# Four graph layers in one launch: when four small loads start, and how the last half of the last layer ends

## The chip, the cores and the metric

The kernel runs on one core of one Trainium2 chip. The metric is the device time of one execution in microseconds (us), and of several executions the median. Before the change it is 2736.38 us, the median of three runs (2735.53 to 2736.8).

## What is computed

Eight graphs (batch B = 8) of N = 2048 nodes with C = 128 features share one adjacency matrix of 2048 x 2048 whole numbers. Four layers follow each other, each on the layer-normed and rectified features, and each adds its output to x. Layers 0, 1 and 3 are graph attention with one score per pair of nodes, layer 2 is attention with four heads and no weights. Cut to what matters here:

```
for layer in 0, 1, 2, 3:
    h = max(layernorm(x), 0)
    x = x + gnn[layer](h, adj)

gnn[3](h):
    h = h * node_weights[n] + node_bias[n] + h
    h = layernorm(h @ W) * gamma + beta
    e = leaky_relu(s1[i] + s2[j], 0.2) where adj[i, j] > 0, else -9e15
    return elu(softmax(e) @ h + h)
```

The four vectors `node_weights`, `node_bias`, `gamma` and `beta` belong to layer 3 alone.

## The kernel before

**Layout.** A graph's x is a tile of 128 partitions x 16 blocks x 128 features. The adjacency is turned once, at the start, into a tile `edge` of bytes (16 blocks of 128 x 2048). Attention runs in *tokens*: for a block `jb` of 128 source nodes and a *half* of 1024 target nodes, VectorE makes the masked weights `zg` (128 x 1024, three buffers; `front`, L758), and PE adds them, in eight groups of 128 columns with two instructions each, against the rows `y` into PSUM (`back`, L767). Column 128 of `y` is a weight, so that the sum by which to divide comes out beside the features. A half has 16 tokens. When the last is done, `out` (L787) divides and ends the half.

**Order.** The instructions of the fast path are put in order by the program itself, one order for each engine. A planner (`Plan`, L171) takes operations with an engine, an estimated duration, a due time, needs, and buffers that they take and free. It simulates them: at each step it takes the engine that can start first, and on it, among the operations that can start within 0.148 us of the first one, that with the lowest due time (a front with free `zg` buffers is ranked 54.8 us earlier). The result is only the order in which each engine gets its instructions. On the chip an engine runs its own in order, and an instruction waits only for the data and buffers that it uses itself. A need that stands in the plan alone is no wait on the chip.

**The start.** SP issues the first graph's x in four loads and then 16 blocks of the adjacency of 1 MB each (L370). Seven buffers take them: five of `z`, two of `m`. VectorE turns each into a block of `edge` (L373), which frees its buffer. Meanwhile the first graph is normed, projected (L590) and its tokens begin (from 29 us). Three more x loads follow the blocks on SP, and ScalarE subtracts 2 from each (L433).

Small loads are issued by GpSimd. `load_weights` (L279) takes weights. `load_more` (L295) takes the four vectors of layer 3: two as 128 x 16 numbers, element by element (`nw1_sb`, `nb_sb`), and two that are spread over all partitions (`gamma_sb`, `beta2_sb`). In the plan it needs the last block of `edge`, `rows_in[NB - 1]` (L1167). The first instructions that read what it loads are at the end of `projections(3)`, in `bounded` (L345, L346), which add 1 to the node weights and double `beta`. `symmetry(j)` (L379) tests on PE and ScalarE that the adjacency is symmetric: block row j against blocks 0 to j of `edge`, and the squares of the differences are summed. In the plan it needs `rows_in[j]`.

**The end of a half in layer 3.** `divided` (L792) takes three banks of PSUM in turn: the reciprocal of the sums (L799), then features times it into `oa` (L800). `rows3` (L811) takes the rows of `y` times `cr[2]`, which gives the normed rows before gamma and beta, into `oe`. `wide3` (L818) adds them to `oa`, multiplies by gamma and adds `beta2_sb`, twice beta, over all 1024 columns. Then ScalarE makes Exp of it into `oe` and Relu in place (L806), and VectorE adds `min(oe, 1)` (L830) and `oa` (L833) to x; the constant -1 that is left over is in x already. SP writes the half to HBM (L925). In halves of the other graphs some of these adds are DMAs of GpSimd (L884, L836). The last half of all is graph 7, half 1; the half before it, graph 7, half 0, shares its buffers `oa` and `oe`, of which there is one each.

Of the kernel before, what the change touches and what calls it, by code (L numbers as in the profile page):

```python
# [8 lines left out]
F32 = mybir.dt.float32  # L9
# [5 lines left out]
AF = mybir.ActivationFunctionType  # L15
OP = mybir.AluOpType
# [4 lines left out]
P = 128  # L21
# [19 lines left out]
def adj_preln_d4(ctx: ExitStack, tc: tile.TileContext, x, adj, w0, a0, w1, a1, w3, a3,  # L41
# [17 lines left out]
    nc = tc.nc  # L59
    B, N, C = x.shape  # L60
    NB = N // P
    HB = NB // 2
    NG = NB // 4
    CE = C + 1
    HN = N // 2
# [16 lines left out]
    edge = const.tile([P, NB, N], U8, name="edge")  # L82
# [9 lines left out]
    nw1_sb = const.tile([P, NB], F32, name="nw1_sb")  # L92
    nb_sb = const.tile([P, NB], F32, name="nb_sb")
    gamma_sb = const.tile([P, C], F32, name="gamma_sb")
    beta2_sb = const.tile([P, C], F32, name="beta2_sb")
# [75 lines left out]
    class Plan:  # L171
# [11 lines left out]
        def add(self, engine, us, due, emit, needs=(), takes=(), frees=(), lag=None, tiled=False):  # L183
            op = Op(engine, us, due, emit, needs, takes, frees, self.LAG[engine] if lag is None else lag, tiled)
            self.ops.append(op)
            return op
# [56 lines left out]
    def fast(ctx):  # L243
        stat = ctx.enter_context(tc.tile_pool(name="stat", bufs=3))
        big = ctx.enter_context(tc.tile_pool(name="big", bufs=2))
        dram = ctx.enter_context(tc.tile_pool(name="dram", bufs=2, space=DRAM))
        ps = ctx.enter_context(tc.tile_pool(name="psum", bufs=1, space=PSUM)).tile(
            [P, 8, 512], F32, name="ps")
# [7 lines left out]
        add = plan.add  # L256
# [36 lines left out]
            load(out=beta_col, in_=beta.rearrange("(p o) -> p o", o=1))  # L293

        def load_more(op):  # L295
            load = nc.gpsimd.dma_start
            load(out=nw1_sb, in_=node_w.rearrange("(n p) -> p n", p=P))
            load(out=nb_sb, in_=node_b.rearrange("(n p) -> p n", p=P))
            load(out=gamma_sb, in_=gamma.partition_broadcast(P))
            load(out=beta2_sb, in_=beta.partition_broadcast(P))  # L300
# [61 lines left out]
        rows_in, squares, loaded = [], [], []  # L362
# [16 lines left out]
        def symmetry(j):  # L379

            wide = (j + 1) * P
            for k in range(0, wide, 512):
                w, n = min(512, wide - k), len(squares)

                def differences(op, k=k, w=w):
                    pv = ps[:, op.got["pair"], :]
                    nc.tensor.matmul(pv[:, :w], lhsT=minus_8, rhs=edge_8[:, j, k:k + w],
                                     start=True, stop=False, skip_group_check=True)
                    for i in range(k // P, (k + w) // P):
                        at = i * P - k  # L390
                        nc.tensor.matmul(pv[:, at:at + P], lhsT=edge_8[:, i, j * P:(j + 1) * P],
                                         rhs=plus_8, start=False, stop=i == (k + w) // P - 1,
                                         skip_group_check=True)

                due = 115.0 + 9.0 * j
                last = add("PE", 0.1 + 0.1 * w / P, due, differences, [rows_in[j], *units[0, 0].v_ready], takes=["pair"])
                squares.append(add("ACT", 0.6, due, lambda op, w=w, n=n, last=last: nc.scalar.activation(
                    ps[:, last.got["pair"], :w], ps[:, last.got["pair"], :w], AF.Square,
                    accum_out=bad[:, n:n + 1]), [last], frees=[("pair", last)]))
# [18 lines left out]
        X, done = {}, {}  # L418
# [19 lines left out]
        class Unit:  # L438
# [81 lines left out]
            def rows_made(self, part, step):  # L520

                key, ends = self.moments("x", 0.0, lambda: X[self.b], [self.after] * 4)
                out, chain = [], []

                def rows(op, q):
# [39 lines left out]
        class Gat(Unit):  # L565
# [221 lines left out]
            def out(self, half, back, place, name, due):  # L787
                layer, b = self.layer, self.b
                hb = slice(half * HB, (half + 1) * HB)
                key = {}  # L790
# [12 lines left out]
                def whole(op, into, func):  # L803
                    if into == "e" and "e" not in key:
                        key["e"] = big.tile([P, HB, C], F32, tag="oe", name="oe", bufs=1)
                    nc.scalar.activation(key[into], key["a"], func)  # L806
# [11 lines left out]
                def wide3(op, k):  # L818
                    a = key["a"]
                    if k == 0:  # L820
                        nc.vector.tensor_add(a, a, key["e"])  # L821
                    elif k == 1:
                        nc.vector.tensor_mul(a, a, gamma_sb[:, None, :].to_broadcast([P, HB, C]))  # L823
                    else:
                        nc.vector.tensor_add(a, a, beta2_sb[:, None, :].to_broadcast([P, HB, C]))  # L825
# [19 lines left out]
                def scaled(op):  # L845
                    key["a"] = big.tile([P, HB, C], F32, tag="oa", name="oa", bufs=1)
                    for i in range(HB):
                        at = i % 3 * CE
                        nc.scalar.activation(key["a"][:, i, :], ps[:, self.banks(half, place)[i // 3], at:at + C], AF.Copy,
                                             scale=key["r"][:, i:i + 1])  # L850

                if layer == 1 and L1_ACT:
                    last = add("DVE", 0.35, due - 30, weights_sums, [back])
                    last = taker = add("ACT", 2.3, due - 30, scaled, [last], takes=["oa"])
                else:
                    last = taker = add("DVE", 1.75, due - 30, divided, [back], takes=["oa"])
# [15 lines left out]
                if layer == 0:  # L872
                    e = e_taker = add("ACT", 0.95, due + 6, lambda op: whole(op, "e", AF.Exp), [last], takes=["oe"])
                    last = add("ACT", 0.95, due + 8, lambda op: whole(op, "a", AF.Relu), [e])
                else:
                    rows = []
                    for k in range(2):
                        rows.append(add("ACT", 1.17, due - 6 + 4 * k, lambda op, k=k: rows3(op, k), rows + [back],
                                        takes=["oe"] if k == 0 else []))
                    e_taker = rows[0]  # L880
                    if not self.left:
                        rows[1].frees.append(("y", self.taker))
                    if L3_DMA and b != B - 1:
                        last = add("POOL", PLUS_US, due + 6, lambda op: nc.gpsimd.dma_start(  # L884
                            out=key["a"], in_=key["e"], accum_op=OP.add), [last] + rows, lag=PLUS_LAG_US)
                    for k in range(L3_DMA and b != B - 1, 3):
                        last = add("DVE", 1.14, due + 6 + 4 * k, lambda op, k=k: wide3(op, k), [last] + rows)
                    e = add("ACT", 0.95, due + 18, lambda op: whole(op, "e", AF.Exp), [last])
                    last = add("ACT", 0.95, due + 20, lambda op: whole(op, "a", AF.Relu), [e])
                late = due + (10 if layer == 0 else 22)  # L890
                if layer == 3 and L3_OUT and b != B - 1:
# [7 lines left out]
                    def plus_out(op, k):  # L899
                        lo = half * HN  # L900
                        nc.gpsimd.dma_start(out=out[b, lo:lo + HN, :].rearrange("(n p) c -> p n c", p=P),
                                            in_=key[k], accum_op=OP.add)

                    written = add("SP", 0.5, due - 10, write_x, done[b, 3], lag=6.0)
                    if not self.left:
                        written.frees.append(("x", x_taken[b]))
                    e = add("DVE", 0.6, late, rest_out, [e])
                    e = add("POOL", PLUS_US, late + 2, lambda op: plus_out(op, "e"), [e, written],
                            frees=[("oe", e_taker)], lag=PLUS_LAG_US)
                    add("POOL", PLUS_US, late + 4, lambda op: plus_out(op, "a"), [e, last],  # L910
                        frees=[("oa", taker)], lag=PLUS_LAG_US)
                    return
                e = add("DVE", 1.14, late, elu_e, [e], frees=[("oe", e_taker)])
                if layer == 0:
                    plus(late + 4, [last, e])
                    return
# [1 line left out]
                if L3_PLUS and b != B - 1:  # L918
                    last = add("POOL", PLUS_US, late + 4, plus_a, [last, e], frees=[("oa", taker)], lag=PLUS_LAG_US)
                else:  # L920
                    last = add("DVE", 1.14, late + 4, elu_a, [last, e], frees=[("oa", taker)])
# [5 lines left out]
                last = add("SP", 0.5, late + 6, write, [last])  # L927
                if not self.left:
                    last.frees.append(("x", x_taken[b]))

        class Heads(Unit):
            def beginning(self):
# [228 lines left out]
        def planned():  # L1161
# [3 lines left out]
            for j in range(NB):  # L1165
                adjacency(j)
            more = add("POOL", 5.0, 55.0, load_more, [rows_in[NB - 1]], lag=6.0)  # L1167
            projected[1] = projections(1, 50.0, [weights, projected[0], *units[0, 0].v_ready])
            projected[3] = projections(3, 55.0, [projected[1], more])
            for j in range(NB):  # L1170
                symmetry(j)
# [35 lines left out]
        units, projected = {}, {}  # L1207
# [171 lines left out]
    with ExitStack() as inner:  # L1379
        inner.enter_context(tc.manual_schedule(engines={  # L1380
            mybir.EngineType.PE, mybir.EngineType.Activation, mybir.EngineType.DVE,
            mybir.EngineType.Pool, mybir.EngineType.SP}))
        fast(inner)
# [28 lines left out]
```

## Time and profile before

| what | value |
|---|---|
| median of three runs | 2736.38 us |
| the profiled execution | 2736.47 us |
| its span in the profile | 2734.70 us |
| granted TensorE clock over the span | 0.992 |
| PE busy | 2624.4 us, 96% |
| VectorE (DVE) busy | 2489.3 us, 91% |
| ScalarE (ACT) busy | 1728.7 us, 63% |
| GpSimd (POOL) busy | 284.4 us, 10% |
| adjacency blocks (`raw`): 16 loads of 1024 KB, issue to landing | 17.0 us, median; 8.2 to 22.9 |
| small loads L297 to L300: issue to landing | 8.1, 8.2, 7.9, 8.5 us |

Busy shares are means over a span in which different stages have different limits. The page also has the span in 40 slices; over a shorter stretch it can be asked again. These are the two rows of the DMA from 0 to 150 us, in slices of 3.75 us; the upper is the busy share of the 16 DMA engines in tenths, the lower what they moved:

```profile
DMA  3999999999999989600000000000005300000000
GB/s 88 295 350 413 295 258 404 417 419 415 419 422 417 366 245 291 187 1 0 0 4 0 2 0 0 4 0 0 0 7 131 149 0 0 7 0 0 0 4 0
```

In a timeline each line is start, duration, engine, source line and operation; the square brackets give how long the engine had been idle and what ended that.

### The profile page before, as it was taken

The numbers are of one execution on the slowest core, as the hardware profiler recorded it, in microseconds if no ns is written. First come the engines' busy times: TensorE is split into PE (matmuls) and PEld (weight loads), VectorE is DVE, ScalarE is ACT, GpSimd is POOL, SyncE is SP. The second block draws the span as 40 slices with busy tenths as digits, with TensorE's granted clock in tenths as the row PEclk, the third lists the DMA queues.
The fourth block names the chain that finished last, engine by engine and source line by source line (L and its number), as shares of the span: only waits on it lengthen the run. The fifth ranks groups of instructions, "written<-read, shape, count | busy, mean of one in ns | idle before, by whom it ended". The sixth has DMA issues, their size and how long they took to land. (4 is left out here: it accounts for less than half of the span.)

```text
span 2734.7 us, 49017 instructions
## 1 busy us (share of the span) xinstructions
PE 2624.4 (96%) x20104; PEld 2017.2 (74%) x20104; DVE 2489.3 (91%) x3304; ACT 1728.7 (63%) x2777; POOL 284.4 (10%) x143
## 2 busy tenths in 40 slices
PE   7999999999999999999999999999999899999997
PEld 6899877857776877766777767777785378666687
DVE  7867989999989999998999989999999689999987
ACT  3524464667676675666856567675655956787651
POOL 1200000111101111010101011011111101101010
PEclk9999999999999999999999999999999999999999
DMA  8003333252344233433443432424234311623121
GB/s 313 17 9 84 72 63 62 47 101 55 61 121 72 61 82 55 82 74 63 86 78 55 93 55 78 89 49 79 48 75 88 62 39 33 131 55 71 35 46 34
DMA packets 216874, 196.48 MB, mean 72 GB/s; under 512 B 142896, under 2 KB 178176, under 8 KB 210496
## 3 DMA queue, kind: packets, MB, share of 16 engines
q1 hardware_dynamic: 144112, 156.46, 22.1%
q0 software_dynamic: 72112, 36.73, 11.6%
q8 instruction: 160, 2.62, 0.4%
q14 instruction: 74, 0.61, 0.1%
q10 hardware_dynamic: 416, 0.07, 0.0%
HBM read 123.03 MB, written 33.73 MB: 57 GB/s over the span
## 5 line engine op out<-in xcount | busy, mean ns | idle before, releaser
L1060 ACT ACTIVATE z<-ps,shift 128x1024 f32<-128x1024 f32 x1024 | 1122.3, 1114 | 700.0 <-PE ps L1053 697.5
L767 PEld LDWEIGHTS ps<-y,zg 128*128 128x128 f32 x12288 | 1461.8, 192 | 76.6 <-DVE zg L758 25.2
L767 PE MATMUL ps<-y,zg 128*128 128x129 f32 x12288 | 1494.5, 276 | 17.6 <-DVE zg L758 10.2
L1066 DVE SCALAR_TENSOR_TENSOR z<-z,edge 128x2048 f32<-128x2048 f32 x512 | 1169.5, 2286 | 72.0 <-ACT z L1060 69.5
L758 DVE SCALAR_TENSOR_TENSOR zg<-r,cr,edge 128x1024 f32<-128x1024 f32 x768 | 969.7, 1278 | 101.3 <-PE ps L767 87.7
L1053 PE MATMUL ps<-m,s 128*128 128x512 f32 x2048 | 717.1, 436 | 48.0 <-ACT z L1060 44.5
L1053 PEld LDWEIGHTS ps<-m,s 128*128 128x128 f32 x2048 | 314.3, 190 | 323.1 <-ACT z L1060 219.5
L1075 PE MATMUL ps<-z,v 128*32 128x512 f32 x4096 | 503.0, 603 | 1.7 <-DVE z L1066 1.4
L1075 PEld LDWEIGHTS ps<-z,v 128*32 128x32 f32 x4096 | 103.8, 109 | 235.9 <-issue 190.5
L529 ACT ACTIVATE h<-x,nmrx,rstdx 128x128 f32<-128x128 f32 x512 | 210.5, 491 | 33.6 <-DVE nmrx L118 26.5
L113 POOL TENSOR_TENSOR rstdx<-varx,neg_half 128x16 f32<-128x16 f32 x31 | 130.1, 4197 | 570.1 <-DVE varx L108 561.0
L836 POOL DMA_DIRECT2D x<-oa x40 | 35.9, 898 | 880.0 <-DVE oa L800 271.4
L1100 POOL DMA_DIRECT2D x<-o x31 | 66.1, 2132 | 516.8 <-DVE o L1095 506.1
L590 PEld LDWEIGHTS ps<-rhs,h_t 128*128 128x128 f32 x768 | 98.5, 193 | 15.5 <-DVE h_t L581 4.5
L590 PE MATMUL ps<-rhs,h_t 128*128 128x130 f32 x768 | 104.0, 279 | 4.6 <-DVE h_t L581 3.4
L462 DVE BATCH_NORM_STATS2 st<-x 128x6 f32<-128x128 f32 x496 | 106.0, 278 | 1.6 <-DMA x<-oa 1.6
L560 PE MATMUL ps<-ident,h 128*128 128x128 f32 x512 | 79.7, 277 | 3.7 <-ACT z L1060 2.8
L581 ACT COPY h_t<-ps 128x512 f32<-128x512 f32 x92 | 53.4, 582 | 40.2 <-PE ps L560 40.0
L800 DVE TENSOR_TENSOR oa<-ps,rs 128x384 f32<-128x384 f32 x144 | 73.8, 513 | 5.1
L560 PEld LDWEIGHTS ps<-ident,h 128*128 128x128 f32 x512 | 62.2, 142 | 19.9 <-ACT z L1060 6.4
L806 ACT ACTIVATE oe<-oa 128x1024 f32<-128x1024 f32 x32 | 33.9, 1059 | 56.8 <-DVE oa L825 54.4
L628 ACT ACTIVATE y<-ps,y 128x128 f32<-128x128 f32 x240 | 68.6, 369 | 0.0
(129 smaller groups left out, 835.3 us busy)
## 6 DMA issues: line engine op xcount, KB each, us to landing
s<-halves SPq DMA_DIRECT2D x256, 128.0 KB, 2.7
m<-halves SPq DMA_DIRECT2D x64, 512.0 KB, 6.9
r<-row SPq DMA_DIRECT2D x42, 512.0 KB, 3.8
x<-oa POOLq DMA_DIRECT2D x40, 512.0 KB, 5.0
raw<-in_adj_dram SPq DMA_DIRECT2D x16, 1024.0 KB, 17.0
values<-h SPq DMA_DIRECT2D x32, 256.0 KB, 2.4
halves<-hi SPq DMA_DIRECT2D x128, 64.0 KB, 1.7
halves<-lo SPq DMA_DIRECT2D x128, 64.0 KB, 1.7
```

The costliest lines, as they stand in the source:

```text
L113: nc.gpsimd.tensor_tensor(out=rstd, in0=v, in1=neg_half, op=OP.pow)
L462: nc.vector.bn_stats(out=key["st"][:, n, :], in_=rows()[:, n, :])
L529: nc.scalar.activation(self.h[q][:, k, :], X[self.b][:, n, :], AF.Relu, scale=key["rstd"][:, n:n + 1], bias=key["nmr"][:, n:n + 1])
L560: nc.tensor.transpose(pk[:, k, :], self.h[q][:, k, :], ident)
L590: nc.tensor.matmul(pv[:, k, :C + 2], lhsT=self.h_t[q][:, k * P:(k + 1) * P], rhs=rhs, start=True, stop=True)
L758: nc.vector.scalar_tensor_tensor(z, self.r[half], self.cr[:, 0, jb:jb + 1], edge[:, jb, half * HN:(half + 1) * HN], op0=OP.max, op1=OP.mult)
L767: nc.tensor.matmul(ps[:, self.banks(half, place)[i // 3], k * CE:(k + 1) * CE], lhsT=z[:, i * P:(i + 1) * P], rhs=self.y[:, jb, :], start= ...
L800: nc.vector.tensor_mul(key["a"][:, i0:i1, :], pv[:, :, :C], r[:, i0:i1, None].to_broadcast([P, i1 - i0, C]))
L1053: nc.tensor.matmul(ps[:, lo + c, :], lhsT=self.S[h, jb // HB][:, at:at + P], rhs=self.M[h][:, (c2 * 2 + c) * 512:(c2 * 2 + c + 1) * 512], ...
L1060: nc.scalar.activation(self.z[s][:, c2 * HN:(c2 + 1) * HN], ps[:, lo:lo + 2, :].rearrange("p b t -> p (b t)"), AF.Exp, bias=shift)
L1066: nc.vector.scalar_tensor_tensor(self.z[s], self.z[s], 1.0, edge[:, jb, :], op0=OP.mult, op1=OP.mult, accum_out=self.den[:, h, jb:jb + 1])
L1075: nc.tensor.matmul(ps[c * HD:(c + 1) * HD, 0, :], lhsT=self.V[h][:, jb, :], rhs=z[:, c * 512:(c + 1) * 512], start=jb == 0, stop=jb == NB - 1,
```

## The change

Four edits. `load_more` gets an instruction ahead of its loads: GpSimd copies one element of the last block of `edge` into `nw1_sb`. The load into `nw1_sb` overwrites it, so it comes after the copy, the copy comes after that block, and the other three loads come after it in GpSimd's order. `symmetry(j)` needs all blocks up to j in the plan. `out` hands the last half of all to a new function, `last_out`. And the operation of `elu_e` is kept under a name, `exp_left`, so that `last_out` can need it (it frees `oe`).

`last_out` makes the rows of that half (`rows3`) as soon as `oe` is free, multiplies them by gamma and adds twice beta (`gain`, `offset`), with due times ahead of the half's last token. After the last token it goes in three parts, of three, three and two blocks, one for each bank of PSUM. For each: reciprocal, then for each block PSUM times reciprocal times gamma, then plus the prepared rows; Exp and Relu on ScalarE; the two adds to x; and a write of its own.

```diff
--- before.py
+++ after.py
@@ -293,6 +293,8 @@
             load(out=beta_col, in_=beta.rearrange("(p o) -> p o", o=1))
 
         def load_more(op):
+
+            nc.gpsimd.tensor_copy(nw1_sb[0:1, 0:1], edge[0:1, NB - 1, 0:1])
             load = nc.gpsimd.dma_start
             load(out=nw1_sb, in_=node_w.rearrange("(n p) -> p n", p=P))
             load(out=nb_sb, in_=node_b.rearrange("(n p) -> p n", p=P))
@@ -393,7 +395,7 @@
                                          skip_group_check=True)
 
                 due = 115.0 + 9.0 * j
-                last = add("PE", 0.1 + 0.1 * w / P, due, differences, [rows_in[j], *units[0, 0].v_ready], takes=["pair"])
+                last = add("PE", 0.1 + 0.1 * w / P, due, differences, [*rows_in[:j + 1], *units[0, 0].v_ready], takes=["pair"])
                 squares.append(add("ACT", 0.6, due, lambda op, w=w, n=n, last=last: nc.scalar.activation(
                     ps[:, last.got["pair"], :w], ps[:, last.got["pair"], :w], AF.Square,
                     accum_out=bad[:, n:n + 1]), [last], frees=[("pair", last)]))
@@ -849,6 +851,9 @@
                         nc.scalar.activation(key["a"][:, i, :], ps[:, self.banks(half, place)[i // 3], at:at + C], AF.Copy,
                                              scale=key["r"][:, i:i + 1])
 
+                if layer == 3 and b == B - 1 and half:
+                    self.last_out(back, due, sums=self.sums_taker[half])
+                    return
                 if layer == 1 and L1_ACT:
                     last = add("DVE", 0.35, due - 30, weights_sums, [back])
                     last = taker = add("ACT", 2.3, due - 30, scaled, [last], takes=["oa"])
@@ -910,7 +915,7 @@
                     add("POOL", PLUS_US, late + 4, lambda op: plus_out(op, "a"), [e, last],
                         frees=[("oa", taker)], lag=PLUS_LAG_US)
                     return
-                e = add("DVE", 1.14, late, elu_e, [e], frees=[("oe", e_taker)])
+                e = self.exp_left = add("DVE", 1.14, late, elu_e, [e], frees=[("oe", e_taker)])
                 if layer == 0:
                     plus(late + 4, [last, e])
                     return
@@ -927,6 +932,71 @@
                 last = add("SP", 0.5, late + 6, write, [last])
                 if not self.left:
                     last.frees.append(("x", x_taken[b]))
+
+            def last_out(self, back, due, sums):
+
+                key = {}
+                def xs(sl):
+                    return X[self.b][:, HB:, :][:, sl, :]
+
+                parts = [slice(0, 3), slice(3, 6), slice(6, 8)]
+
+                def rows3(op, k):
+                    if k == 0:
+                        key["e"] = big.tile([P, HB, C], F32, tag="oe", name="oe", bufs=1)
+                    for i in range(k * 4, k * 4 + 4):
+                        n = HB + i
+                        nc.scalar.activation(key["e"][:, i, :], self.y[:, n, :C], AF.Copy, scale=self.cr[:, 2, n:n + 1])
+
+                def gain(op):
+                    nc.vector.tensor_mul(key["e"], key["e"], gamma_sb[:, None, :].to_broadcast([P, HB, C]))
+
+                def offset(op):
+                    nc.vector.tensor_add(key["e"], key["e"], beta2_sb[:, None, :].to_broadcast([P, HB, C]))
+
+                def divided(op, g):
+                    if g == 0:
+                        key["a"] = big.tile([P, HB, C], F32, tag="oa", name="oa", bufs=1)
+                        key["r"] = stat.tile([P, HB], F32, tag="rs", name="rs")
+                    sl = parts[g]
+                    n = sl.stop - sl.start
+                    pv = ps[:, self.banks(1, 0)[g], :n * CE].rearrange("p (k c) -> p k c", c=CE)
+                    nc.vector.reciprocal(key["r"][:, sl], pv[:, :, C])
+                    for k in range(n):
+                        i = sl.start + k
+                        nc.vector.scalar_tensor_tensor(key["a"][:, i, :], pv[:, k, :C], key["r"][:, i:i + 1], gamma_sb,
+                                                       op0=OP.mult, op1=OP.mult)
+                    nc.vector.tensor_add(key["a"][:, sl, :], key["a"][:, sl, :], key["e"][:, sl, :])
+
+                def part(op, g, into, func):
+                    sl = parts[g]
+                    nc.scalar.activation(key[into][:, sl, :], key["a"][:, sl, :], func)
+
+                def elu(op, g, of, op0, scalar):
+                    sl = parts[g]
+                    nc.vector.scalar_tensor_tensor(xs(sl), key[of][:, sl, :], scalar, xs(sl),
+                                                   op0=op0, op1=OP.add)
+
+                def write(op, g):
+                    sl = parts[g]
+                    nc.sync.dma_start(out=out[self.b, HN:, :].rearrange("(n p) c -> p n c", p=P)[:, sl, :],
+                                      in_=xs(sl))
+
+                ahead = []
+                for k in range(2):
+                    ahead.append(add("ACT", 1.17, due - 25 + k, lambda op, k=k: rows3(op, k),
+                                     ahead + [self.powers, self.exp_left],
+                                     takes=["oe"] if k == 0 else []))
+                last = add("DVE", 1.15, due - 20, gain, ahead)
+                last = add("DVE", 1.14, due - 20, offset, [last])
+                for g in range(3):
+                    last = add("DVE", 1.45, due, lambda op, g=g: divided(op, g), [back, last],
+                               takes=["oa"] if g == 0 else [])
+                    e = add("ACT", 0.4, due, lambda op, g=g: part(op, g, "e", AF.Exp), [last])
+                    a = add("ACT", 0.4, due, lambda op, g=g: part(op, g, "a", AF.Relu), [e])
+                    e = add("DVE", 0.48, due + 1, lambda op, g=g: elu(op, g, "e", OP.min, 1.0), [e])
+                    a = add("DVE", 0.48, due + 1, lambda op, g=g: elu(op, g, "a", OP.add, 0.0), [e, a])
+                    add("SP", 0.6, due, lambda op, g=g: write(op, g), [a])
 
         class Heads(Unit):
             def beginning(self):
```

## The prediction

> **What bounds the kernel now.** The change touches two short stretches, the start (to about 75 us) and the last half (from 2698 us), so the page's whole-span shares (PE 96%, DVE 91%) say little about it. I read the page's row of DMA rate in slices first. It falls from 413 GB/s to 295 and 258 between 15 and 22.5 us and comes back to 404, while the DMA engines stay at nine tenths busy. Then I asked for busy time by stage (columns after the stretch: PE, PEld, DVE, ACT and POOL busy, granted clock, DMA share, GB/s), and for the DMA queues of the same two stretches (packets, MB, share of 16 engines):
>
> ```profile
> 16.00:23.00 7.00, 4.59 (x36) 3.72 (x34) 5.44 (x7) 4.77 (x12) 0.00 (x0) 1.00 1.01 249
> 23.00:30.00 7.00, 4.01 (x19) 3.44 (x19) 4.56 (x7) 1.32 (x4) 0.00 (x0) 0.52 1.02 425
> ```
> ```profile
> q1 hardware_dynamic: 215, 1.60, 85.3%
> q0 software_dynamic: 155, 0.15, 15.7%
> ...
> q1 hardware_dynamic: 406, 2.97, 101.8%
> ```
>
> In the first seven microseconds q1, which carries the adjacency blocks, moved 1.60 MB, in the next seven 2.97 MB. What is in the way is q0, with only 0.15 MB. Its traffic is found on GpSimd's timeline, and what it delays on VectorE's:
>
> ```profile
> 11.57 1.56 POOL L297 DMA_DIRECT2D nw_sb<-_L_gnn_node_weights_dram  x1
> 13.13 1.15 POOL L298 DMA_DIRECT2D nb_sb<-in_L_gnn_node_bias_dram  x1
> 14.27 1.18 POOL L299 DMA_DIRECT2D gamma_sb<-in_L_gnn_ln_gamma_dram  x1
> 15.45 0.54 POOL L300 DMA_DIRECT2D beta_sb<-in_L_gnn_ln_beta_dram  x1
> 80.92 6.95 POOL L113 TENSOR_TENSOR rstdx<-varx,neg_half 128x16 f32<-128x16 f32 x2 [64.93 <-DVE varx L108]
> ```
> ```profile
> 11.12 1.23 DVE L373 TENSOR_SCALAR edge<-raw 128x2048 uint8<-128x2048 int32 x1 [0.85 <-DMA raw<-in_adj_dram]
> 13.65 1.68 DVE L373 TENSOR_SCALAR edge<-raw 128x2048 uint8<-128x2048 int32 x1 [0.20 <-DMA raw<-in_adj_dram]
> ...
> 21.09 1.23 DVE L373 TENSOR_SCALAR edge<-raw 128x2048 uint8<-128x2048 int32 x1 [0.96 <-DMA raw<-in_adj_dram]
> ...
> 24.98 1.23 DVE L373 TENSOR_SCALAR edge<-raw 128x2048 uint8<-128x2048 int32 x1 [2.07 <-DMA raw<-in_adj_dram]
> ...
> 36.66 1.23 DVE L373 TENSOR_SCALAR edge<-raw 128x2048 uint8<-128x2048 int32 x1 [1.96 <-DMA raw<-in_adj_dram]
> ```
>
> So the plan puts `load_more` after the last block, but nothing in the program makes GpSimd wait: the small loads start at 11.57 and land 7.9 to 8.5 us after issue, in the middle of the blocks. From 37 us edges and tokens follow each other on VectorE without a wait on PE or data until 54 us, and from 39 us PE is nearly always busy. Whatever the third, fifth and ninth waits lose is not won back later.
>
> The end, in the timelines of PE, VectorE and ScalarE:
>
> ```profile
> 2703.61 16.35 PE L767 MATMUL ps<-y,zg 128*128 128x129 f32 x144 [0.28 <-DVE zg L758]
> ```
> ```profile
> 2702.28 4.87 DVE L758 SCALAR_TENSOR_TENSOR zg<-r,cr,edge 128x1024 f32<-128x1024 f32 x4
> 2707.49 1.28 DVE L758 SCALAR_TENSOR_TENSOR zg<-r,cr,edge 128x1024 f32<-128x1024 f32 x1 [0.34 <-PE ps L767]
> ...
> 2718.88 0.18 DVE L799 RECIPROCAL rs<-ps 128x3 f32<-128x3 f32 x1 [2.96 <-PE ps L767]
> 2719.10 0.56 DVE L800 TENSOR_TENSOR oa<-ps,rs 128x384 f32<-128x384 f32 x1
> ...
> 2727.23 1.23 DVE L833 SCALAR_TENSOR_TENSOR x<-oa,x 128x1024 f32<-128x1024 f32 x1
> ```
>
> The last matmul ends at 2718.86 by the chain of waits. After it comes a serial chain of 9.60 us to 2728.46; the write is issued at 2728.48, lands 3.7 us later (2732.2), and the span ends 2.5 us after that.
>
> **The small loads.** One GpSimd copy of one element is added; the nearest row, the same kind at L999, is 0.17 us. It waits for the last edges, 54.09 + 1.23 = 55.3 now. Behind it on GpSimd are the four issues (3.9 us to the start of the fourth) and then nothing until 80.92, with 64.93 us idle before. SP is not passed. The gain at the blocks, three ways. By bytes: 2.97 - 1.60 = 1.37 MB at 2.97/7 = 0.424 MB/us is 3.2 us. By arrivals: blocks 0 and 1 came 2.5 us apart, which puts block 4 at 11.1 + 4 x 2.5 = 21.1; it came at 24.98, 3.9 us late. By VectorE's waits: 0.96 + 2.07 + 1.96 = 5.0 us, the most that can go. I take **3.5 us**, between the two that measure the DMA itself; 3.2 and 5.0 are the ends. VectorE and PE can follow: with no wait for data, the edges now at 27.46 would come at about 24.4, because projections and copies between them need nothing else that is late.
>
> [...] The row decides: q1 lost 1.37 MB. Half of these loads goes in runs of 4 bytes (a guess at why).
>
> The loads now meet the three x loads instead, whose traffic ends at about 63 us. That would end 3.5 earlier and be held up by as much, so again at about 63; ScalarE needs the third x at 65.82 + 2 x 1.93 - 3.5 = 66.2. Covered by 3 us. The readers of the small loads are L345 and L346:
>
> ```profile
> 73.27 0.17 DVE L345 TENSOR_SCALAR nw_sb<-nw_sb 128x16 f32<-128x16 f32 x1
> 73.35 0.22 DVE L346 TENSOR_SCALAR beta_sb<-beta_sb 128x128 f32<-128x128 f32 x1
> ```
>
> The last issue would start at 51.8 + 0.2 + 3.9 = 55.9 and land 8.5 later, at 64.4; L346 would come at 69.85. Cover 5.4 us; without it, VectorE stands still, and all fronts behind it.
>
> **The symmetry edit** only adds earlier blocks to the plan's needs. The squares of later blocks run up to 20 us and more after the last edges, so the order should not move: 0. If it did, 0.4 us pieces of PE would change place, at most some tenths either way.
>
> **The end.** Removed behind the last matmul: three adds and multiplies over the whole half, 3 x 1.26 = 3.8 us from start to start; the rows on ScalarE ran ahead already (2700.06 to 2702.51). Added ahead: gain and offset, 2 x 1.14 us (start to start, as between fronts), as soon as the rows are there. Their due times are lower than the fronts', so one goes after the front of 2702.28 and one a front later. Fronts eight and nine of the half (counting from zero) are then done at 2705.9 and 2708.2. PE wants them at 2705.4 and 0.5 + 2707.2: two waits of 0.5 us. After that VectorE has 0.5 us to spare per token. Cost **1.1 us**; ends 0 (both put where three fronts are in store) and 1.7 (one put a front earlier).
>
> Then per part of three blocks: reciprocal 0.22, three 128-wide multiplies (384-wide 0.56 and 256-wide 0.42 give 0.28 each by their difference, 0.19 from start to start) 0.66, an add of 384 columns 0.5: 1.4 us. By the plan's order (part 0, part 1, e of 0, part 2, a of 0, e of 1, e of 2, a of 1, a of 2, each elu 0.43 from start to start, 0.35 for two blocks) the last elu ends 6.1 us after the first reciprocal starts; ScalarE's 0.47 per half-step (its 384-wide row) lies beside it. The second and third writes go out at 5.9 and 6.3. The row of 512 KB has its packets from 0.9 us after issue for 1.9 us, and lands 0.6 after them: the third lands at 8.4, against 13.3 now. Gain 4.9, net of PE **3.8 us**. [...] But rows of 64 KB and 256 KB to DRAM land in 1.7 and 2.4 us and are issued 0.4 apart[...]. Ends of the net gain: 2.5 (each short instruction at full duration, 0.7 more, and PE at 1.7) and 5.0.
>
> **Sum.** 3.5 + 3.8 = 7.3. The profiled execution took 2736.47 (span 2734.70 plus 1.77), 0.09 above the median of 2736.38: 2736.4 - 7.3 = **2729.1 us**. [...] I let the shift of the start pass whole. A measurement here can tell 0.2%, 5.5 us, from no change: the line is 2730.9. Forecast's own range: 5.7 to 10, 2726.4 to 2730.7; chance 0.58.
>
> **Rivals.**
> - *The start's gain does not pass on* (another wait, such as the clock of 0.52 of that stretch or a later fixed arrival, takes its place). For: PE stood at half clock there; against: no row between 39 and 75 us waits for anything but its neighbours. Only the end counts: 2732.6. Chance 0.16.
> - *The end is spent again*: PE pays all 2.4 us for gain and offset and the parts line up at their full latencies, end about -1. For: 0.5 us of slack per token; against: three buffers of store. 2731.9. Chance 0.11.
> - *The wait shows in full*: VectorE's waits for blocks go entirely, 5.0 + 3.8: 2727.6. Chance 0.10.
> - *Slower: the small loads arrive late at L346.* They decide from a landing after 69.85, and the kernel is slower than before from 14 + 7.3 = 21.3 us after issue. For: adjacency blocks took up to 22.9 us to land in this trace, the x loads 19.1. At 22.9 us: 78.8, 9.0 late, 2738.1. Against: with seven blocks outstanding q0 still landed in 8.5. Chance 0.05.
>
> Faster 0.67 (forecast but for its edge, and the third), same 0.28, slower 0.05. The range, 2727.0 to 2732.8, takes in both partial cases.
>
> **What will show it.** DMA rate near 420 between 16 and 23 us and the edges after 20 us without waits of 1 us; L345 about 3.5 us earlier and without idle time before it; GpSimd's four issues at 52 to 57; in the last half two PE waits of half a microsecond; the last VectorE instruction 6 us after the first reciprocal. Wrong if L345 waits for DMA, if the edges still wait beyond 20 us, or if tokens elsewhere stand in another order.

## The result, and the profile after

Over 20 executions each the changed kernel took 2732.3 us in the median and the kernel before 2736.58; the ratio is 0.9982 with a 95% interval of 0.9976 to 0.9988, so 4.9 us less (3.3 to 6.6). The two medians alone differ by 4.3. The prediction was 2729.1 with a range of 2727.0 to 2732.8. The direction and this range held, but the gain forecast was 7.3. The measured one lies outside the range of the forecast proper (5.7 to 10 us), and just short of the 0.2% (5.5 us) that I had set as the least a measurement here can tell from no change, though its interval leaves out zero. The profiled execution has a span of 2729.5 us, 5.2 less than before.

**The start.** GpSimd's timeline of the changed kernel from 9 to 75 us:

```profile
50.97 1.16 POOL L297 CAST nw_sb<-edge 1x1 f32<-1x1 uint8 x1 [38.51 <-DVE edge L375]
52.43 1.22 POOL L299 DMA_DIRECT2D nw_sb<-_L_gnn_node_weights_dram  x1 [0.30 <-POOL nw_sb L297]
53.65 1.15 POOL L300 DMA_DIRECT2D nb_sb<-in_L_gnn_node_bias_dram  x1
54.79 0.56 POOL L301 DMA_DIRECT2D gamma_sb<-in_L_gnn_ln_gamma_dram  x1
55.34 0.54 POOL L302 DMA_DIRECT2D beta_sb<-in_L_gnn_ln_beta_dram  x1
```

The copy of one element waits for the last edges, as meant, and the four loads now stand behind it, 41 us later than before (52.43 against 11.57). Only the first of them writes the tile of the copy; the other three start behind it in GpSimd's order, at 53.65, 54.79 and 55.34. In busy time by stage (same columns as before the change), and on VectorE's timeline:

```profile
16.00:23.00 7.00, 6.12 (x36) 5.53 (x35) 5.63 (x8) 4.82 (x13) 0.00 (x0) 1.00 1.02 422
```
```profile
21.00 1.22 DVE L375 TENSOR_SCALAR edge<-raw 128x2048 uint8<-128x2048 int32 x1
...
22.73 1.22 DVE L375 TENSOR_SCALAR edge<-raw 128x2048 uint8<-128x2048 int32 x1
...
32.13 1.23 DVE L375 TENSOR_SCALAR edge<-raw 128x2048 uint8<-128x2048 int32 x1 [0.22 <-DMA raw<-in_adj_dram]
...
68.86 0.17 DVE L347 TENSOR_SCALAR nw_sb<-nw_sb 128x16 f32<-128x16 f32 x1
68.94 0.22 DVE L348 TENSOR_SCALAR beta_sb<-beta_sb 128x128 f32<-128x128 f32 x1
```

The DMA moves 422 GB/s where it moved 249. The DMA queue of the blocks in the same 7 us:

```profile
q1 hardware_dynamic: 408, 2.96, 101.7%
```

Before, 155 packets of the small loads (q0) took only 15.7% of the engines' time, and yet q1 moved 215 packets instead of 408. Most of the loss stands in the blocks' own packets: of much the same size (7.3 to 7.4 KB), they took about 0.44 us each before (85.3% of 16 engines x 7 us, over 215) and 0.28 after. What made them longer beside the small loads no run shows.

The edges that had waited 0.96, 2.07 and 1.96 us wait 0, 0 and 0.22. The readers of the small loads come at 68.86 and 68.94, 4.4 us sooner, with no idle time in front of them: the loads had landed 7.3 to 8.7 us after issue, the last at 62.6.

**The end.** PE from the first matmul of the last half, VectorE from that half's rows to the last division, and the three writes (duration in ns of their issue; landing in us):

```profile
2686.24 9.21 PE L769 MATMUL ps<-y,zg 128*128 128x129 f32 x80 [0.33 <-DVE oa L802]
...
2700.38 2.05 PE L769 MATMUL ps<-y,zg 128*128 128x129 f32 x16 [0.28 <-DVE zg L760]
2702.71 2.05 PE L769 MATMUL ps<-y,zg 128*128 128x129 f32 x16 [0.28 <-DVE zg L760]
2705.04 12.77 PE L769 MATMUL ps<-y,zg 128*128 128x129 f32 x112 [0.28 <-DVE zg L760]
```
```profile
2700.24 1.22 DVE L952 TENSOR_TENSOR oe<-oe,gamma_sb 128x1024 f32<-128x1024 f32 x1
2701.37 1.28 DVE L760 SCALAR_TENSOR_TENSOR zg<-r,cr,edge 128x1024 f32<-128x1024 f32 x1
2702.57 1.22 DVE L955 TENSOR_TENSOR oe<-oe,beta_sb 128x1024 f32<-128x1024 f32 x1
...
2716.73 0.18 DVE L964 RECIPROCAL rs<-ps 128x3 f32<-128x3 f32 x1 [2.96 <-PE ps L769]
2716.95 0.87 DVE L967 SCALAR_TENSOR_TENSOR oa<-ps,rs,gamma_sb 128x128 f32<-128x128 f32 x3
2717.85 0.56 DVE L969 TENSOR_TENSOR oa<-oa,oe 128x384 f32<-128x384 f32 x1
2718.32 0.17 DVE L964 RECIPROCAL rs<-ps 128x3 f32<-128x3 f32 x1
...
2722.84 0.88 DVE L977 SCALAR_TENSOR_TENSOR x<-oa,x 128x384 f32<-128x384 f32 x2
```
```profile
L982 SPq DMA_DIRECT2D out_dram<-x x3: 372/373/442, 2722.1 to 2723.9; - x3
...
DMA to landing us min/median/max: 2.1/2.4/2.8
```

The stretch of nine tokens that ran through before (144 instructions without a break) is cut into 16, 16 and 112: two tokens go at VectorE's pace, 2.33 us from start to start, where the 144 took 16.35 / 9 = 1.82 each. From the first reciprocal to the end of the span it is 2729.5 - 2716.73 = 12.8 us, against 15.8 before.

Two measures serve below, because they scatter much less than the total. One is the start of the instruction that doubles beta; over the nine executions in which all four loads were held back it lies between 68.84 and 69.60. The other runs from the first matmul of the last half (the 80 instructions that wait 0.33 us for `oa`) to the end of the span: 2734.7 - 2689.47 = **45.2** before, 2729.5 - 2686.24 = **43.3** after. It repeats within 0.15 us where the end is the same. Its line before:

```profile
2689.47 9.21 PE L767 MATMUL ps<-y,zg 128*128 128x129 f32 x80 [0.33 <-DVE oa L800]
```

### The profile page after: what moved, and what is told of

Its sections match the earlier page's. It is cut to its first block, busy times and chain, and to the rows that moved or that the text cites. A ratio compares the mean times of both kernels' runs of the same rounds, so it can differ in the third digit from the quotient of the medians.

```text
span 2729.5 us, 49035 instructions
## 1 busy us (share of the span) xinstructions
PE 2625.8 (96%) x20104; PEld 2019.7 (74%) x20104; DVE 2489.2 (91%) x3315; ACT 1729.0 (63%) x2781; POOL 285.8 (10%) x144
## 4 chain that ended last, share of the span: by engine, by line
## 6 DMA issues: line engine op xcount, KB each, us to landing
raw<-in_adj_dram SPq DMA_DIRECT2D x16, 1024.0 KB, 15.5
```

## The experiments

Theory: the change makes two gains that have nothing to do with each other, some 4 us at the start from the one wait on GpSimd, and 2 us at the end. Rivals: that the symmetry edit or the order of the plan has a part in it, that the end gains nothing, and that of the small loads the larger ones do the harm. All results together; the last column is the ratio to the kernel before with its 95% interval, where enough executions were timed; the other kernels ran once, and a single total scatters too much to be used:

| kernel | beta doubled at | last half, first matmul to end | ratio to before |
|---|---|---|---|
| before | 73.35 | 45.2 | |
| changed | 68.94 | 43.3 | 0.9982 (0.9976 to 0.9988) |
| changed, again | 69.38 | 43.3 | 0.9985 (0.9977 to 0.9992) |
| guard alone | 69.08 | 45.3 | 0.9989 (0.9981 to 0.9997) |
| end alone | 72.49 | 43.3 | 0.9993 (0.9985 to 1.0001) |
| only the single numbers late | 69.77 | 45.2 | |
| only the spread rows late | 71.91 | 45.1 | |
| parts alone | 69.08 | 44.9 | |
| ahead alone | 69.57 | 44.5 | |
| pieces later | 69.46, again 69.03 | 42.3, again 42.2 | 0.9971 (0.9959 to 0.9983) |
| ScalarE divides, first form | 68.84 | 42.7 | |
| ScalarE divides, second form | 69.60 | 41.9 | 0.9975 (0.9966 to 0.9983) |

**The guard alone, and the end alone.** The first is the kernel before with one line more, and without the symmetry edit:

```diff
         def load_more(op):
+            nc.gpsimd.tensor_copy(nw1_sb[0:1, 0:1], edge[0:1, NB - 1, 0:1])
             load = nc.gpsimd.dma_start
```

> The kernel before with the guard ahead of the four small loads and nothing else. My theory: the whole gain of the start is this one wait, so VectorE doubles beta at 68.9 us (73.35 before, 68.94 after the whole change), and the end is as before: 15.8 us from the first reciprocal of the last half to the end of the span. Total 3.3 to 4.4 us below before. Rival (the gain of the start needs the plan's new needs of the symmetry test, or is lost again before the end in every execution): 73.3 us at that marker, or 68.9 there and a total within 1 us of before.

The second is the changed kernel without that line.

> The changed kernel without the guard. My theory: the start is as before (beta doubled at 73.3 us), PE loses 1.1 us in the last half to two waits, and from the first reciprocal to the end of the span it takes 12.8 us instead of 15.8: 2.0 us below before in all. Rival (the end's gain is spent, and what the changed kernel won is the start alone): within 0.5 us of before in the last 45 us of the span.

The two markers and the stretch of 23 to 30 us, first in the guard alone, then in the end alone:

```profile
69.08 0.22 DVE L347 TENSOR_SCALAR beta_sb<-beta_sb 128x128 f32<-128x128 f32 x1
...
2686.33 9.21 PE L768 MATMUL ps<-y,zg 128*128 128x129 f32 x80 [0.33 <-DVE oa L801]
```
```profile
23.00:30.00 7.00, 4.83 (x30) 4.37 (x29) 6.97 (x12) 1.69 (x6) 0.00 (x0) 0.81 1.01 419
```
```profile
72.49 0.22 DVE L347 TENSOR_SCALAR beta_sb<-beta_sb 128x128 f32<-128x128 f32 x1
...
2690.88 9.21 PE L768 MATMUL ps<-y,zg 128*128 128x129 f32 x80 [0.33 <-DVE oa L801]
```
```profile
23.00:30.00 7.00, 2.85 (x22) 2.36 (x21) 5.71 (x9) 1.85 (x9) 0.00 (x0) 1.00 1.01 400
```

The guard alone moved the marker to 69.08 and left the last half at 45.3. The end alone took 43.3 there and left the start without the guard's gain: 72.49, with waits of 0.61, 1.22 and 0.84 us for blocks. That is 0.9 sooner than the 73.3 expected; the small loads began at 13.05 in that execution instead of 11.57, and whether this is scatter or the plan's order is open. The ratios are 3.0 us less (0.8 to 5.2) and 1.9 us less (4.1 less to 0.3 more). The sum, 4.9, is what the whole change gives. So the gains are separate and the symmetry edit is not needed for the first one. Both rivals fall, that of the end by its stretch of the trace rather than by its time, whose interval holds zero. The total of the guard alone came out a little short of what I expected, inside the scatter, and its interval leaves out zero: the start's gain does pass on.

The clock of that stretch, which the prediction named as a thing that might take the wait's place, has no such part. The end alone was granted 1.00 from 23 to 30 us and its marker came late; the guard alone was granted 0.81 and came early.

**Which of the small loads.** Each of these two is the kernel before with the loads in two groups and the guard between them. The first:

```diff
+            load(out=gamma_sb, in_=gamma.partition_broadcast(P))
+            load(out=beta2_sb, in_=beta.partition_broadcast(P))
+            nc.gpsimd.tensor_copy(nw1_sb[0:1, 0:1], edge[0:1, NB - 1, 0:1])
             load(out=nw1_sb, in_=node_w.rearrange("(n p) -> p n", p=P))
             load(out=nb_sb, in_=node_b.rearrange("(n p) -> p n", p=P))
-            load(out=gamma_sb, in_=gamma.partition_broadcast(P))
-            load(out=beta2_sb, in_=beta.partition_broadcast(P))
```

> The kernel before; of the four small loads, the two that are spread over the partitions (gamma, beta, 128 KB in SBUF) go first and early, and the guard holds back only the two of 2048 single numbers (16 KB). If the runs of 4 bytes are what holds up the blocks (my theory, by two thirds or more), beta is doubled at 69 to 70.5 us and the rate from 16 to 23 us stays above 370 GB/s. If the spread rows do (rival, they have most of the bytes), it stays at 72 to 73.3 us.

The second leaves the loads in their order and has the guard behind the first two.

> The counterpart: the two loads of single numbers early, the guard ahead of the two spread ones. My theory (runs of 4 bytes): beta is doubled at 72 to 73.3 us, rate from 16 to 23 us below 320 GB/s. Rival (spread rows): 69 to 70.5 us.

With the single numbers late the marker stands at 69.77, with the spread rows late at 71.91. Busy time by stage, first with the single numbers late, then with the rows late, there with the DMA queues:

```profile
16.00:23.00 7.00, 6.22 (x34) 5.92 (x32) 5.59 (x8) 4.42 (x9) 0.00 (x0) 1.00 1.01 389
```
```profile
16.00:23.00 7.00, 6.22 (x30) 5.82 (x29) 4.94 (x7) 4.71 (x12) 0.00 (x0) 1.00 1.02 282
...
q1 hardware_dynamic: 269, 1.96, 96.4%
q0 software_dynamic: 96, 0.02, 5.3%
```

Against 73.35 the single numbers are worth 3.6 of the 4.4 us and the rows 1.4; against the 72.49 of the other execution without a guard, 2.7 and 0.6. Either way, the 16 KB in runs of 4 bytes hold the blocks up more than the 128 KB in runs of 512 bytes. With the single numbers early, q0 moved 0.02 MB in 5.3% of the engines' time, and the blocks still had only 282 GB/s. Each of the two is one execution; they show which loads cost, not that it is the length of the runs rather than the number of pieces. The second marker lies 0.1 below its expected band; the order of the two is clear.

**The end taken apart.** In one kernel the rows are not prepared, and each part does everything after the last matmul:

```diff
-                last = add("DVE", 1.15, due - 20, gain, ahead)
-                last = add("DVE", 1.14, due - 20, offset, [last])
...
+                    nc.vector.tensor_mul(a, pv[:, :, :C], key["r"][:, sl, None].to_broadcast([P, n, C]))
+                    nc.vector.tensor_add(a, a, key["e"][:, sl, :])
+                    nc.vector.tensor_mul(a, a, gamma_sb[:, None, :].to_broadcast([P, n, C]))
+                    nc.vector.tensor_add(a, a, beta2_sb[:, None, :].to_broadcast([P, n, C]))
```

> The changed kernel, but nothing of the last half's rows is multiplied or offset ahead: each of the three parts does reciprocal, multiply, plus rows, times gamma, plus twice beta. My theory: the two PE waits of 0.28 us and the slower pace behind them are gone, so PE ends the last half 1.1 us sooner than in the changed kernel, but VectorE has 9.1 us of work behind it instead of 7.0, and from the first reciprocal to the end of the span it takes 14.9 us (changed kernel 12.8, before 15.8). Rival (the parts are what pays, and work ahead is not needed, since ScalarE is the one to wait for): 12.8 to 13.3 us and PE sooner.

In the other the rows are prepared, but there is one part, `parts = [slice(0, 8)]`, and one write:

> The changed kernel with its rows prepared ahead, but one part and one write. My theory: PE has the same two waits as in the changed kernel, and from the first reciprocal to the end of the span it takes 14.1 us (3.0 for the divisions in 128-wide pieces, 1.26 for the add, 1.1 for Exp, 2.5 for two adds to x, 6.2 for the write of 512 KB and what follows it). Rival (the three writes cost more than they save): 12.8 us or less.

From the first reciprocal to the end: 2729.1 - 2713.65 = 15.5 us with parts alone (14.9 expected: an add or multiply that needs the one before it starts 0.59 to 0.66 us after it, where independent ones of 384 columns start 0.47 apart, so that VectorE ends after 9.6 us and not 9.1) and 2727.0 - 2712.98 = 14.0 with the rows ahead alone (14.1 expected). Parts alone have no extra PE wait. Over the whole last half they gain 0.4 and 0.7 us, and together 2.0: work ahead takes VectorE's load off the end (in the changed kernel it ends 7.0 us after the first reciprocal, with parts alone 9.6), and parts let ScalarE and the write run beside what is left (in the changed kernel from 1.8 and 5.4 us after it). The 0.7 is what is left after the two PE waits; without them it would be about 1.8, an estimate (15.8 - 14.0) that no run tested.

**Pieces placed later.** The prediction held that the gain and offset cost PE 1.1 us only because they stand too early. Here they come in four pieces of 256 columns, one behind each of fronts 10 to 13 (counted from zero):

```diff
-                last = add("DVE", 1.15, due - 20, gain, ahead)
-                last = add("DVE", 1.14, due - 20, offset, [last])
+                for k in range(4):
+                    last = add("DVE", 0.75, due - 20, lambda op, k=k: prepared(op, k), ahead + [self.fronts[NB + 10 + k]])
```

> The changed kernel, with gain and offset in four pieces of 256 columns, one behind each of the fronts 10 to 13 of the last half, where VectorE waits for PE and three fronts are in store. My theory: VectorE has 0.5 us per token to spare there and 2 us in store, the pieces take 0.75 each, so PE has no wait more than before the change and ends 1.1 us sooner against the half before than in the changed kernel; 12.8 us from the first reciprocal to the end stay. Rival (the store is less than I think, or the cuts cost more): PE waits between fronts 11 and 15 and nothing is won.

> The changed kernel with gain and offset in four later pieces, timed. My theory: 42.3 us from the first matmul of the last half to the end of the span, and about 1.0 us below the changed kernel in the median, which the scatter between executions may hide. Rival: no difference in that stretch (43.3 us).

PE and VectorE of its first execution:

```profile
2684.97 9.21 PE L769 MATMUL ps<-y,zg 128*128 128x129 f32 x80 [0.33 <-DVE oa L804]
...
2699.10 16.35 PE L769 MATMUL ps<-y,zg 128*128 128x129 f32 x144 [0.28 <-DVE zg L760]
```
```profile
2704.54 0.42 DVE L955 TENSOR_TENSOR oe<-oe,gamma_sb 128x256 f32<-128x256 f32 x1
2704.99 0.42 DVE L956 TENSOR_TENSOR oe<-oe,beta_sb 128x256 f32<-128x256 f32 x1
2705.34 1.28 DVE L760 SCALAR_TENSOR_TENSOR zg<-r,cr,edge 128x1024 f32<-128x1024 f32 x1
...
2714.37 0.18 DVE L965 RECIPROCAL rs<-ps 128x3 f32<-128x3 f32 x1 [2.58 <-PE ps L769]
```

The stretch of 144 is whole again. The waits of half a microsecond for PE that VectorE had at every front are gone, filled by the pieces. From the first matmul of the half to the first reciprocal it is 2714.37 - 2684.97 = 29.4 us, as before the change (29.4); the changed kernel takes 30.5. The end of 12.9 us stays. Timed together with the changed kernel, it is 2729.63 us in the median against 2733.44: a ratio to before of 0.9971 (0.9959 to 0.9983) against 0.9985 (0.9977 to 0.9992). The intervals overlap; the 1.0 us is shown by the trace, not by the times. The rest of the difference has no stretch of a trace behind it, and I take it for scatter.

**ScalarE divides two parts.** On top of the pieces, ScalarE makes PSUM times reciprocal for the five blocks of parts 1 and 2, while VectorE does part 0:

```diff
+                def scaled(op, g):
+                    for k in range(parts[g].stop - parts[g].start):
+                        i = parts[g].start + k
+                        nc.scalar.activation(key["a"][:, i, :], columns(g)[:, k, :C], AF.Copy, scale=key["r"][:, i:i + 1])
```

> As the kernel with pieces placed later, and ScalarE divides the five blocks of parts 1 and 2 while VectorE does part 0. My theory: behind the last matmul VectorE is the bound (7.0 us without a gap in the changed kernel), and its work falls to 6.2, so 12.0 us from the first reciprocal to the end. Rival (the chain through ScalarE and the writes is the bound): 12.8 us or more.

A miss: 12.6 us from the first reciprocal, and 42.7 from the first matmul, more than without it. Its reciprocals began with the bank of part 1. That first reciprocal comes 30.1 us after the first matmul of the half instead of 29.4, because PE finishes the banks in their order (0.7 us later, not the 0.4 that the next expectation names). The second form does part 0 first:

> As the kernel with later pieces; VectorE does part 0 at once, then the reciprocals of parts 1 and 2, whose five blocks ScalarE divides. In the earlier form of this VectorE began with the bank of part 1, which PE finishes 0.4 us after that of part 0. My theory: VectorE is the bound, with 6.3 us of work instead of 7.0, so 12.2 us from the first reciprocal to the end and 41.7 us from the first matmul of the last half. Rival (the chain through ScalarE, now longer, is the bound): 42.3 us or more.

It took 2728.3 - 2715.82 = 12.5 us, and 41.9 from the first matmul: 0.3 to 0.4 us better than the pieces alone, and half of what was expected, because VectorE now stands 0.44 us waiting for ScalarE's divisions. Both theories have a part. In time it is not told apart from the pieces alone (0.9975, 0.9966 to 0.9983).

**The changed kernel again**, timed beside the pieces and the second form:

> The changed kernel again, to be compared with the kernel before and with the two others of this call. 0.1 to 0.25% faster than before, as when it was first measured; 43.3 us from the first matmul of the last half to the end of the span (45.2 before); beta doubled at 68.5 to 69.5 us.

All three came as expected: 0.15%, 43.3 and 69.38.

## Why the prediction was right, and where it was wrong

- *The sum, 7.3:* its two terms were 3.5 and 3.8, and the traces show 4.4 and 2.0. One error is 0.9 too small and one 1.8 too large, and they cancel in part. The measured 2732.3 lies closest to the totals of two rivals, 2732.6 (the start's gain does not pass on) and 2731.9 (the end is spent again), and the wide range was drawn to take in both. So the total alone would not have told the forecast from them, and that the range held is partly its width. That both gains are there is shown by the traces.
- *What bounds the start:* right. The adjacency blocks were late because of four small loads that nothing held back: with the guard alone the rate from 16 to 23 us is 419 GB/s instead of 249. (The edges that waited were the fourth, fifth and ninth; the prediction's "third" is a slip.)
- *3.5 us at the start:* too small. The profile shows 4.4, and with the guard the marker stood at 68.8 to 69.6 in nine executions, against 73.35 and 72.49 without: 2.9 to 4.5. I took a value between the loss in bytes and the delay of block 4. The delay of a block was nearer, and VectorE's waits, 5.0, nearly all went.
- *"q1 lost 1.37 MB":* right. It now moves 2.96 MB in those 7 us instead of 1.60. The bytes of the small loads do not explain it: at the 0.424 MB/us of the stretch after, their 0.15 MB would be 0.35 us (an estimate). Of what I called a guess, that runs of 4 bytes are what costs, the runs show this much: the loads that have them make most of it (2.7 to 3.6 us, against 0.6 to 1.4 for the spread rows).
- *The x loads and L345 as cover:* right. The readers did not wait, and the slower rival had no part.
- *The copy at 0.17 us:* wrong and harmless. It took 1.16 and a pause of 0.30, on an engine with nothing else to do.
- *The symmetry edit at 0:* right. The guard alone, without it, moved the start as much.
- *Two PE waits, 1.1 us:* right. From the first matmul of the half to the first reciprocal it is 30.5 instead of 29.4, and moving the work later took just that away.
- *"The third lands at 8.4, against 13.3 now. Gain 4.9":* this is the step that failed, in size. The end took 12.8 us from the first reciprocal instead of 10.9 (8.4 plus the 2.5 behind the landing), for three reasons. Divisions of 128 columns out of PSUM with three operands last 0.345 us each, not 0.28 by the difference of two wider rows without the third operand; three of them take 0.87 and a part 1.59 instead of 1.4. With six short adds at up to 0.47 from start to start, VectorE ends after 7.0 us, not 6.1. And the third write, issued at 7.2, landed 2.8 us later, not 2.1: 10.0 instead of 8.4. I had counted its packets alone, but they follow those of the second write, issued 0.46 us before it, in one stretch of some 1.3 us. (The 0.9 + 1.9 + 0.6 that I took from the row of 512 KB is also 0.3 short of its 3.7.) The remaining 0.3 lies behind the landing. Net of PE the end gives 2.0 us, below the 2.5 that I had set as its lower end. "Each short instruction at full duration, 0.7 more" was meant as the bad case; the instructions did overlap and VectorE still lost 0.9, because the durations themselves were taken too short.
- *The rows of 64 and 256 KB for the split:* the reading from them was right. One behind the other, with the first issued at 5.4 us and the measured 2.1, 2.4 and 2.8 us to landing, the three writes would have ended 12.7 us after the first reciprocal (an estimate); the third was issued at 7.2, while the second was still under way (it landed at 9.1), and landed at 10.0.
- *"I let the shift of the start pass whole":* not so in a single pair of executions. In the profiled ones, 4.4 us at 69 us had become 3.2 at the first matmul of the last half (2689.47 to 2686.24). Over many executions, 4.4 + 2.0 = 6.4 lies near the upper end of the measured 3.3 to 6.6 and just outside the 2.2 to 6.3 of the repeat. From one marker to the other it is 2616.1 us before and 2618.4 in the end alone, both without the guard, and 2612.9 to 2623.3, 2616.9 in the mean, in the nine with it. So no loss shows there, but this stretch scatters by more than the gain, and whether part of it is lost on average was not settled.

## What to carry to other kernels

A planner's need is not a wait on the chip: a load that is planned late but waits for nothing goes out early (here at 11.57 us, ahead of the last edges at 54.09), and two loads of 16 KB in all, in runs of 4 bytes, held up the megabytes that everything waits for by 2.7 to 3.6 us. Work that is prepared ahead was free here only where VectorE really waited (29.4 us from the first matmul to the first reciprocal, against 30.5 with the same work earlier), so look for the place with full buffers and a recurring gap; here it lay three fronts on from where due times put it. For short instructions take the duration from a row of the same shape and operands: here the difference of two wider rows with one operand less gave 0.28 for a measured 0.345, and how much of that is the width and how much the operand was not told apart.

## What the runs showed of the hardware

How much a single execution of the same instructions differs was not expected: 2727 to 2738 us for the changed kernel. The time goes with the mean granted clock. Over the 45 executions of the kernel before that were timed beside the repeat, the correlation is -0.81, and 0.001 less of the clock goes with 2.0 us more. Busy time by stage shows where the clock goes. The same place of the program, in the changed kernel and in the one with parts alone, whose order is the same there (the column after POOL is the granted clock):

```profile
549.90:553.30 3.40, 1.76 (x7) 0.93 (x7) 2.49 (x2) 2.88 (x4) 0.00 (x0) 0.99 0.82 174
553.30:556.70 3.40, 3.40 (x12) 1.21 (x16) 3.07 (x6) 2.96 (x3) 0.00 (x0) 0.51 0.58 153
556.70:566.90 10.20, 7.83 (x44) 3.11 (x37) 8.75 (x18) 6.79 (x8) 0.00 (x0) 1.00 1.08 202
```
```profile
549.90:553.30 3.40, 1.92 (x6) 0.97 (x6) 2.83 (x3) 2.89 (x4) 0.00 (x0) 1.00 0.68 151
553.30:556.70 3.40, 3.27 (x21) 1.10 (x21) 3.29 (x7) 2.08 (x3) 0.00 (x0) 1.00 0.69 191
```

After a stretch in which PE is busy for about half the time (1.76 and 1.92 of 3.4 us), one execution is granted half the clock for 3.4 us (0.51 in the mean) and the other is not (1.00); PE then gets 12 instructions done instead of 21. One such stretch takes 1.7 us of full clock, 0.0006 of the mean, so about 1.2 us by the slope above, an estimate. What decides which of the two happens no run shows. That such stretches set the gain in single executions is inferred from these rows and the correlation; no run held the clock fixed.
